# Five edits to the first part of a sparse graph-attention kernel: shared buffers, later degree counts, v beside A, a column-wise split, deeper loads

**Chip, cores, metric.** One core of a Trainium2 chip; the batches of runs used several chips, each with the kernel before beside it. The metric is the device time of one execution in microseconds (us). Lower is better.

## What the kernel computes

The reference is one graph-attention layer over 3327 nodes with 1024 features. It is cut here to what matters:

```python
h = jnp.maximum(_layernorm(x, axis=-1), 0.0)          # x: 3327 x 1024, float32
f = h @ Wf + bf
g = h @ Wg + bg
e = jax.nn.relu(f @ g.T)
scores = jnp.where(adj > 0, e, NEG)                    # adj: 3327 x 3327, int32, about 17 ones a row
attention = jax.nn.softmax(scores, axis=1)
x = x + attention @ (h @ W + bW)
```

Of the kernel before, what the change touches and what calls it, by code (L numbers as in the profile page):

```python
# [26 lines left out]
AHEAD = 3  # L27

# [260 lines left out]
def edge_path(ctx: ExitStack, tc: tile.TileContext, x, adj, Wf, bf, Wg, bg, W, bW, out, flag):  # L289
# [46 lines left out]
    sel3 = const.tile([3, 3], FP, name="sel3")  # L336
    make_identity(nc, sel3)
# [13 lines left out]
    def split3(pool, to, of):  # L351

        n = of.shape[1]
        rest = pool.tile([3, n], FP, name="rest")
        tc.keep_in_program_order(nc.vector.tensor_copy(rest, of))
        part = pool.tile([3, n], BF, name="part")
        acc = pool.tile([3, n], FP, name="part_acc")
        for i in range(3):
            nc.vector.tensor_copy(part, rest)
            if i == 0:  # L360
                nc.vector.tensor_scalar(acc, part, sel3[:, 0:1], None, op0=ALU.mult)
            else:
                nc.vector.scalar_tensor_tensor(acc, part, sel3[:, i : i + 1], acc, op0=ALU.mult, op1=ALU.add)
            if i < 2:
                nc.vector.tensor_sub(rest, rest, part)
        nc.vector.tensor_copy(to, acc)


    with ExitStack() as part1:
        pool1 = lambda name, bufs, **kw: part1.enter_context(tc.tile_pool(name=name, bufs=bufs, **kw))  # L370
        c1 = pool1("c1", 1)
        wrow = pool1("wrow", 2)
        wT = pool1("wT", 2)
        ln = pool1("ln", 3)
        lnj = pool1("lnj", 1)
        apool = pool1("adj", 2)
        kpool = pool1("key", 2)
# [4 lines left out]
        p_lst = pool1("p_lst", 1, space=PSUM)  # L382
        p_c = pool1("p_c", 1, space=PSUM)

# [5 lines left out]
        iotad = p_c.tile([P, NBIN], FP, name="iotad")  # L390
# [10 lines left out]
        deg = c1.tile([P, NT], FP, name="deg")  # L401
        cnt = c1.tile([P, NT], FP, name="cnt")
# [39 lines left out]
        def degrees(t):  # L442
            n = rows(t)
            a = apool.tile([P, N], I32, name="a")
            for b, m in pieces(t):
                nc.sync.dma_start(a[b : b + m], adj[t * P + b : t * P + b + m, :])
            r = kpool.tile([P, N], FP, name="r")
            nc.scalar.activation(r[:n], a[:n], AF.Relu, accum_out=deg[:n, t : t + 1])  # L448
            nc.gpsimd.tensor_mul(r[:n], r[:n], iotaj[:n])  # L449
            return r  # L450

        def edges(t, r):

# [9 lines left out]
            lst = p_lst.tile([P, KM], FP, name="lst")  # L463
# [9 lines left out]
            nc.vector.tensor_scalar(oh[:n, t, :], iotad[:n], dg[:n], None, op0=ALU.is_equal)  # L473

# [29 lines left out]
        bf3 = c1.tile([P, KD, 3], FP, name="bf3")  # L504
        bWf = c1.tile([3, O], FP, name="bWf")
        nc.gpsimd.dma_start(bfT, bf.rearrange("(k p) -> p k", p=P))
        nc.gpsimd.dma_start(bgT, bg.rearrange("(k p) -> p k", p=P))
        nc.gpsimd.dma_start(bWf, bass.AP(tensor=bW.tensor, offset=bW.offset, ap=[[0, 3], [1, O]]))
        nc.vector.tensor_copy(bf3, bfT[:, :, None].to_broadcast([P, KD, 3]))
# [6 lines left out]
        def make_A(c):  # L516
# [15 lines left out]
            nc.scalar.copy(A_sb[:, c, D : D + 1], ps[:, 0:1])  # L532

        def make_rows():

            ps = p_u.tile([P, P], FP, name="ps_u")
            for k in range(KD):
                nc.tensor.matmul(ps[:3, 0:1], bf3[:, k, :], bgT[:, k : k + 1], start=(k == 0), stop=(k == KD - 1))
            split3(c1, v3[:, D : D + 1], ps[:3, 0:1])
            for o in range(OH):  # L540
                ps = p_mm.tile([P, CB], FP, name="ps_A")
                for k in range(KD):
                    nc.tensor.matmul(  # L543
                        ps[:3], bf3[:, k, :], WgT[:, k, o * CB : (o + 1) * CB], start=(k == 0), stop=(k == KD - 1)
                    )
                split3(c1, v3[:, o * CB : (o + 1) * CB], ps[:3])
                split3(c1, bW3[:, o * CB : (o + 1) * CB], bWf[:, o * CB : (o + 1) * CB])

        for t in range(NT):
            r = degrees(t)  # L550
            normed(t)
            edges(t, r)
# [4 lines left out]
            elif t < 2 * KD:  # L557
                make_A(t - KD)
# [292 lines left out]
```

## The kernel before

The kernel does not compute 3327 x 3327 scores. Its first part goes once through the rows, in 26 tiles of 128. For each tile it normalises the rows of x and writes them to `hd` in DRAM. It also loads the rows of adj and turns them into "keys" (adj times column number). From these VectorE picks the neighbours' column numbers with Max8 instructions, eight largest values at a time, up to 40 a row. Beside that PE builds A = Wf Wg^T, so that a score becomes one dot product of (h A + v) with a neighbour's h. At the end of the first part the rows are sorted by degree; the sorted order is `perm`. The second part gathers each row's neighbours, computes the scores, the softmax and the output. The change leaves the second part alone.

The pieces of the first part that matter, with cuts marked by `# ...`:

```python
wrow = pool1("wrow", 2)
ln = pool1("ln", 3)          # row buffers: xt and its small companions
apool = pool1("adj", 2)
kpool = pool1("key", 2)
# ...
def normed(t):
    xt = ln.tile([P, D], FP, name="xt")
    # nc.sync.dma_start: load of x
    if t % 2:                                   # odd tiles: statistics on VectorE
        st = ln.tile([P, D // CB, 6], FP, name="st")
        for c in range(D // CB):
            nc.vector.bn_stats(st[:n, c, :], xt[:n, c * CB : (c + 1) * CB])
        mv = ln.tile([P, 2], FP, name="mv")
        nc.vector.bn_aggr(mv[:n], st[:n])
        nc.scalar.activation(nmr[:n], mv[:n, 0:1], AF.Copy, scale=-1.0)
        nc.scalar.activation(rstd[:n], mv[:n, 1:2], AF.Sqrt, bias=eps[:n])
    else:                                       # even tiles: two passes on ScalarE
        # ...
    nc.vector.reciprocal(rstd[:n], rstd[:n])
    nc.scalar.activation(nmr[:n], nmr[:n], AF.Copy, scale=rstd[:n])
    nc.scalar.activation(xt[:n], xt[:n], AF.Relu, bias=nmr[:n], scale=rstd[:n])
    # nc.scalar.dma_start: store to hd

def degrees(t):
    a = apool.tile([P, N], I32, name="a")
    # nc.sync.dma_start: load of adj
    r = kpool.tile([P, N], FP, name="r")
    nc.scalar.activation(r[:n], a[:n], AF.Relu, accum_out=deg[:n, t : t + 1])   # "the adj pass"
    nc.gpsimd.tensor_mul(r[:n], r[:n], iotaj[:n])                               # "the multiply"
    return r

def edges(t, r):
    for s in range(SEG):                                                        # "the scans"
        nc.vector.max(cand[:n, s * 8 : s * 8 + 8], r[:n, s * SW : min(N, (s + 1) * SW)])
    # ... list work on VectorE; then a product on PE and a masked sum on VectorE (rp)

for t in range(NT):
    r = degrees(t)
    normed(t)
    edges(t, r)
    # ... store_lists
    if t < KD:
        load_Wg(t)
    elif t < 2 * KD:
        make_A(t - KD)
# ... sort by degree, giving perm and final
make_rows()      # v on three partitions, and split3 of v and bW into three bf16 parts
```

Each engine gets its instructions in an order that is fixed when the kernel is built. "Emitted earlier" below means earlier in the program. The build interleaves neighbouring pieces. So where the order matters, it is read from a timeline.

## Time and profile before

| | before |
|---|---|
| median of 3 runs | 1437.71 us (1436.15 to 1441.19) |
| profiled run, span | 1436.2 us |
| first scan | 20.6 us |
| loop end (start of the prefix scan after the last tile) | 277.4 us |
| permutation known | 290.8 us |
| first gathered dot | 329.9 us |
| first dot to end | 1106.3 us |

These milestones are start times in the timeline of the profiled run and are used all through. The prediction below shows the stretches, the waits and the chain of the kernel before. Each line of a timeline is: start (us), duration (us), engine, line, operation, output<-inputs, shapes, and in brackets how long the engine idled before and who released it.

### The profile page before, as it was taken

Reading aid. Unit: us, or ns where it says so; the run is one execution under the profiler, and the core shown is the slowest. Engines: PE = TensorE matmul, PEld = TensorE weight load, DVE = VectorE, ACT = ScalarE, POOL = GpSimd, SP = SyncE. Lnnn points to the kernel's source line nnn. Section 1 sums busy time; section 2 is a strip of 40 time slices with the busy share of each in tenths; the row PEclk is TensorE's granted clock in tenths of the full one; section 3 lists DMA queues with packets and bytes.
Section 4 is the critical chain, followed back from the end, with each engine's and each line's share of the span. In section 5 each row is a group of like instructions: output and inputs, shape, how many; then the busy total and the mean of one; then the engine's idle time right before and its main releaser. Section 6 shows DMA issues by size and latency. Waiting matters only on the chain.

```text
span 1436.2 us, 13878 instructions
## 1 busy us (share of the span) xinstructions
PE 1160.7 (81%) x4242; PEld 657.3 (46%) x4242; DVE 1266.7 (88%) x2647; ACT 442.7 (31%) x673; POOL 873.6 (61%) x627
## 2 busy tenths in 40 slices
PE   1249899457087998999979888999999998999676
PEld 1225454034063665556455444555555554555332
DVE  3878888977979999998988889999999988999991
ACT  6666757301060444324122221222222111111100
POOL 8676776426756677665575556666676765666500
PEclk9999899769588999999989898999999998999788
DMA  8898887249768888896796668887787776787700
GB/s 340 292 348 294 325 302 260 86 140 402 236 224 310 310 315 276 302 314 206 279 324 210 230 261 281 292 286 271 266 287 258 257 254 228 252 275 256 263 30 32
DMA packets 97709, 372.51 MB, mean 259 GB/s; under 512 B 14265, under 2 KB 14681, under 8 KB 94297
## 3 DMA queue, kind: packets, MB, share of 16 engines
q0 software_dynamic: 79552, 286.86, 57.6%
q1 hardware_dynamic: 10860, 70.49, 13.4%
q10 hardware_dynamic: 7212, 14.18, 2.6%
q8 instruction: 35, 0.57, 0.2%
q14 instruction: 50, 0.41, 0.1%
HBM read 343.68 MB, written 27.80 MB: 259 GB/s over the span
## 4 chain that ended last, share of the span: by engine, by line
PE 35%; DVE 27%; issue 18%; POOL 10%; DMA 6%; ACT 3%; POOLq 0%; ACTq 0%; SPq 0%; DVEq 0%
PE ps_o L749 16%; DVE y L735 12%; PE ps_q L655 10%; POOL r L449 6%; DVE junk L672 5%; PE yT_ps L713 5%; DMA G<-hd,pi 4%; POOL G L627 4%; DVE cand L458 3%; PE ps_A L525 2%; ACT r L448 1%; PE ps_A L543 1%; DVE xp L757 1%; DVE sc L672 1%; DVE lst L465 1%
## 5 line engine op out<-in xcount | busy, mean ns | idle before, releaser
L627 POOL DMA_INDIRECT G<-hd,pi x468 | 560.8, 1198 | 316.6 <-ACT y L733 99.1
L672 DVE CUSTOM_DVE_ANT_0 junk<-G,q 128x1024 bf16<-128x1024 f32 x468 | 600.7, 1284 | 31.5 <-DMA G<-hd,pi 28.8
L655 PE MATMUL ps_q<-A_sb,hT 128*128 128x342 f32 x1248 | 394.5, 466 | 63.5 <-ACT q L657 53.5
L735 DVE SCALAR_TENSOR_TENSOR y<-G,sc,y 128x1024 f32<-128x1024 f32 x320 | 411.3, 1285 | 4.7 <-ACT y L733 2.9
L749 PE MATMUL ps_o<-W_sb,yT 128*128 128x512 f32 x832 | 387.1, 620 | 9.8 <-ACT yT L744 9.5
L655 PEld LDWEIGHTS ps_q<-A_sb,hT 128*128 128x128 f32 x1248 | 233.2, 194 | 183.4 <-ACT q L657 55.6
L749 PEld LDWEIGHTS ps_o<-W_sb,yT 128*128 128x128 f32 x832 | 161.0, 198 | 207.9 <-issue 189.1
L449 POOL TENSOR_TENSOR r<-r,iotaj 128x3327 f32<-128x3327 f32 (+1 forms) x26 | 187.8, 7232 | 73.1 <-ACT r L448 61.5
L458 DVE MAX8 cand<-r 128x8 f32<-128x208 f32 (+2 forms) x416 | 134.1, 361 | 39.8 <-POOL r L449 39.8
L657 ACT COPY q<-ps_q 128x342 f32<-128x342 f32 x78 | 32.8, 449 | 328.7 <-DVE sc L672 225.2
L729 ACT ACTIVATE G<-G,sc 128x1024 f32<-128x1024 f32 x122 | 129.0, 1136 | 0.0
L525 PE MATMUL ps_A<-WgT,WfT 128*128 128x512 f32 x256 | 120.3, 630 | 2.9 <-ACT WfT L499 2.9
L713 PE MATMUL yT_ps<-ident,G 128*128 128x128 f32 x976 | 116.4, 275 | 1.3 <-ACT G L729 1.3
L713 PEld LDWEIGHTS yT_ps<-ident,G 128*128 128x128 f32 x976 | 106.7, 141 | 13.2 <-ACT G L729 5.9
L639 ACT COPY hT<-ps_t 128x512 f32<-128x512 f32 x52 | 30.1, 593 | 192.1 <-PE ps_q L655 159.8
L744 ACT COPY yT<-yT_ps 128x512 f32<-128x512 f32 x52 | 27.8, 586 | 199.1 <-PE yT_ps L713 199.1
L525 PEld LDWEIGHTS ps_A<-WgT,WfT 128*128 128x128 f32 x256 | 50.8, 202 | 74.1 <-issue 64.7
L448 ACT ACTIVATE r<-a 128x3327 f32<-128x3327 int32 (+1 forms) x26 | 77.2, 2968 | 9.5 <-issue 5.4
L713 PE MATMUL yT_ps<-ident,y 128*128 128x128 f32 x208 | 33.8, 316 | 56.6 <-DVE y L735 35.7
L758 POOL DMA_INDIRECT out_dram<-xp,perm x25 | 31.7, 1268 | 56.9 <-DVE xp L757 50.9
L757 DVE TENSOR_TENSOR xp<-ps_o,xp 128x512 f32<-128x512 f32 x52 | 35.6, 685 | 34.2 <-PE ps_o L750 34.0
L713 PEld LDWEIGHTS yT_ps<-ident,y 128*128 128x128 f32 x208 | 28.0, 163 | 61.4 <-DVE y L735 38.5
(137 smaller groups left out, 748.7 us busy)
## 6 DMA issues: line engine op xcount, KB each, us to landing
a<-in_adj_dram SPq DMA_DIRECT2D x25, 1663.5 KB, 9.1
xt<-in_x_dram SPq DMA_DIRECT2D x25, 512.0 KB, 4.2
hd<-xt ACTq DMA_DIRECT2D x25, 512.0 KB, 5.6
G<-hd,pi POOLq DMA_INDIRECT x468, 6.1
wr<-in_L_gnn_Wg_dram SPq DMA_DIRECT2D x8, 512.0 KB, 6.0
wr<-in_L_gnn_Wf_dram SPq DMA_DIRECT2D x8, 512.0 KB, 5.0
W_sb<-in_L_gnn_W_dram SPq DMA_DIRECT2D x1, 4096.0 KB, 14.2
a<-in_adj_dram SPq DMA_DIRECT2D x1, 1455.6 KB, 9.6
```

Of the source, the lines that this page charges most:

```text
L448: nc.scalar.activation(r[:n], a[:n], AF.Relu, accum_out=deg[:n, t : t + 1])
L449: nc.gpsimd.tensor_mul(r[:n], r[:n], iotaj[:n])
L458: nc.vector.max(cand[:n, s * 8 : s * 8 + 8], r[:n, s * SW : min(N, (s + 1) * SW)])
L525: nc.tensor.matmul(ps, WfT[:, k, :], WgT[:, k, o * CB : (o + 1) * CB], start=(k == 0), stop=(k == KD - 1))
L627: nc.gpsimd.indirect_dma_start(out=to, out_offset=None, in_=table, in_offset=bass.IndirectOffsetOnAxis(ap=idx, axis=0),)
L655: nc.tensor.matmul(ps[:, :QB], hT[:, k, :], A_sb[:, k, o : o + QB], start=(k == 0), stop=False)
L672: nc.vector.tensor_tensor_reduce(junk, g, e["q"][:, :D], 1.0, e["q"][:, D : D + 1], op0=ALU.mult, op1=ALU.add, accum_out=e["sc"][:, k : k ...
L713: nc.tensor.matmul(e["yT"][:, c, :], g[:, c * P : (c + 1) * P], ident, is_transpose=True, start=(first and c % 4 == 0), stop=(last and c % ...
L729: nc.scalar.activation(g, g, AF.Copy, scale=p)
L735: nc.vector.scalar_tensor_tensor(y, g, p, y, op0=ALU.mult, op1=ALU.add)
L749: nc.tensor.matmul(ps, yT[:, k, :], W_sb[:, k, o * CB : (o + 1) * CB], start=(k == 0), stop=False)
L757: nc.vector.tensor_add(xo, e["o"][o], xo)
```

## The change

The intent is to let the loop run nearer to its engines' own limits, and to take a tail of small work off the path after the loop:

- adj and key share four buffers, so the adj pass works in place;
- the product and masked sum of a tile's degrees come four tiles after its list (`LAG = 4`);
- v is made along with A as columns, and the split into bf16 parts works on 17 columns of 128 partitions at tile 16, where it worked on rows of three partitions after the loop;
- the last two tiles run adj pass and multiply in halves;
- five row buffers in place of three, three weight-row buffers in place of two.

```diff
+LAG = 4
-        wrow = pool1("wrow", 2)
+        wrow = pool1("wrow", 3)
-        ln = pool1("ln", 3)
+        ln = pool1("ln", 5)
-        apool = pool1("adj", 2)
-        kpool = pool1("key", 2)
+        kpool = pool1("key", 4)
@@ degrees
-            a = apool.tile([P, N], I32, name="a")
+            r = kpool.tile([P, N], FP, name="r")
+            a = r.bitcast(I32)
-            nc.scalar.activation(r[:n], a[:n], AF.Relu, accum_out=deg[:n, t : t + 1])
-            nc.gpsimd.tensor_mul(r[:n], r[:n], iotaj[:n])
+            cuts = [0, SEG // 2 * SW, N] if t >= NT - 2 else [0, N]
+            for i, (b, e) in enumerate(zip(cuts, cuts[1:])):
+                to = deg[:n, t : t + 1] if not i else half[:n]
+                nc.scalar.activation(r[:n, b:e], a[:n, b:e], AF.Relu, accum_out=to)
+                nc.gpsimd.tensor_mul(r[:n, b:e], r[:n, b:e], iotaj[:n, b:e])
# ... (deg plus half)
@@ make_A
+            for k in range(KD):
+                nc.tensor.matmul(
+                    v_ps[:, c : c + 1], WgT[:, k, c * P : (c + 1) * P], bfT[:, k : k + 1],
+                    start=(k == 0), stop=(k == KD - 1),
+                )
@@ make_rows
# ... (split3 on 3 partitions removed)
+            for i in range(3):
+                nc.vector.tensor_copy(terms[:, i, :], cols)
+                if i < 2:
+                    nc.vector.tensor_sub(cols, cols, terms[:, i, :])
# ... (17 small products bring the parts back to three partitions)
@@ loop
             edges(t, r)
+            if t >= LAG:
+                counted(t - LAG)
# ...
+            if t == 2 * KD:
+                make_rows()
@@ after the sort
-        make_rows()
```

## The prediction, made before the changed kernel ran

> **What bounds the kernel now.** I read the page first, for the engines' shares over the 40 slices; then the table of busy time by stretches, to split the run; then the waits of the first 305 us, those of the DMA queues included; then the chain and the timeline around the end of the first part.
>
> The change touches only the first part (lists of neighbours, layer norm, A = Wf Wg^T, the permutation), which ends near 290 us; the first gathered dot of the second part starts at 329.88 us. The rest, 330 to 1436 us, runs the same code after the change. In the table of stretches the columns are PE, PEld, DVE, ACT, POOL (busy us and instructions), the granted clock, the share of the DMA engines and GB/s:
>
> ```profile
> 90.00:110.00 20.00, 13.34 (x28) 5.52 (x27) 14.32 (x73) 11.23 (x20) 14.45 (x2) 1.00 0.87 334
> 130.00:150.00 20.00, 18.84 (x69) 10.00 (x67) 16.45 (x83) 13.55 (x21) 14.45 (x2) 1.00 0.90 337
> 190.00:210.00 20.00, 19.79 (x65) 10.16 (x65) 14.03 (x67) 13.93 (x22) 12.24 (x2) 1.00 0.70 256
> 290.00:305.00 15.00, 0.92 (x25) 0.74 (x23) 13.27 (x35) 0.00 (x0) 4.08 (x4) 0.50 0.42 140
> ```
>
> No engine is full in the loop over the 26 row tiles. VectorE has 194.8 us of work in the 240 us from 30 to 270 us (sum over the stretches), 81%, at a period of 10 us per tile: 8.1 us of work a tile. GpSimd shows two multiplies of 7.23 us in most stretches of 20 us (14.45, x2). The DMA engines' share times 20 us, summed over 0 to 270 us, gives 217 us. So three resources could each go faster than 10 us a tile (8.1, 7.2, and 217/26 = 8.35 us), and something couples them. The waits say what (total us, times, longest; SPq is the queue that issues the loads of adj, x and the weights, in order):
>
> ```profile
> SPq L417 <- DMA hd<-xt: 147.3, 18, 15.9
> POOL r L449 <- ACT r L448: 61.5, 18, 8.1
> DVE cand L458 <- POOL r L449: 39.8, 17, 3.9
> ACT nmr L437 <- DVE rstd L436: 30.1, 11, 4.7
> ACT nmr L426 <- DVE mv L425: 16.4, 7, 4.2
> SPq L610 <- DVE bW L366: 24.7, 1, 24.7
> ```
>
> The load of x (L417) stands 147 of the loop's some 260 us until an old row buffer has been stored to hd: there are three such buffers. All later loads, adj included, stand behind it. A ring follows: store of hd, load of x, statistics on VectorE, ScalarE's nmr and its adj pass, GpSimd's multiply, the Max8 scans on VectorE, the next layer norm. The last row is a second matter, after the loop. VectorE then splits two rows of three partitions into bf16 parts; the memory of the first part is not free until that ends. The chain there (start, us, what):
>
> ```profile
> 287.77 0.78 DVE place L585
> 289.03 1.32 PE ps_u L591 x26
> 290.92 0.55 PE ps_u L538 x16
> 293.21 0.61 DVE rest L355
> ...
> 304.25 0.61 DVE rest L355
> 304.95 1.94 PE ps_t L638 x8
> 306.89 6.70 PE ps_q L655 x16
> ```
>
> The permutation is known at 290.8 us, yet the transposes of the first gathered rows start at 304.95[...]. The split as a whole runs until 315.3, and only then does the gather of the lists start:
>
> ```profile
> 315.58 0.95 POOL L627 DMA_INDIRECT pi<-pd,perm  x1 [7.13 <-DVE bW L366]
> ...
> 322.20 0.94 POOL L627 DMA_INDIRECT G<-hd,pi  x1 [3.17 <-issue]
> ```
>
> [...]the stretches here reach 374 GB/s at a share of 0.96, so the measurement puts the ceiling near 390 and I use the shares. [...]a subtraction on 3x512 takes 0.67 us[...], one on 3x1 0.14 us. So 17 columns on 128 partitions must be near the small end.
>
> **The change part by part.**
>
> *Five row buffers, three weight-row buffers.* The load of x waits for a store two tiles older than now, some 20 us earlier at the present period. The longest such wait is 15.9 us, so it should nearly vanish, and with it the queueing of adj loads.
>
> *Shared adj/key buffers.* Two adj plus two key buffers become four that serve both, the same memory. A buffer is held from the issue of its load to the last Max8: 9.1 us landing (12 when several loads are queued, my estimate), 3.2 ScalarE, 7.3 GpSimd with up to 4 of waiting, 5.5 for the scans mixed with list work: 25 to 32 us. Over four buffers that is 6.3 to 8 us a tile: just enough, without much to spare.
>
> *Degree counts four tiles behind.* The product of tile t with the triangle and its masked sum move behind the list of tile t+4. VectorE waits 7.8 us in all for that product and PE 43.8 us for its input, as PE works off A in blocks of 14 to 16.8 us. No instruction vanishes. I count 5 of VectorE's 45 us of loop idle here.
>
> *v along with A.* The row form took 32 products of 676 ns on PE (17.4 us). It becomes 64 fp32 products with one moving column, 128 records; the like-shaped group for u (128x1, x128) is busy 14.7 us with the records overlapping. PE in the loop is thus 3 us lighter or equal. PE is nearly full from 110 to 250 us (18.6 of 20), but starts A only near 98 us, when all of Wg has landed. With faster loads I put that at 70 to 75 us. Eight blocks of 18.5 us plus 1.8 each take 163 us: A ends near 235, before the loop does. So PE is not the bound, by 10 us or so.
>
> *Column-wise split at tile 16.* The split took 291.5 to 315.3 us, 23.8 us of VectorE. It becomes five operations on 17 columns, some 0.2 us each by the small ones above, plus six ScalarE copies (0.6 us at most each) and 17 small products, all inside the loop. VectorE gains 23 us; how much is on the path must be worked out (below).
>
> *Last two tiles in halves.* The scans of the last tile could start 3.6 us earlier (half of 7.21). But VectorE is busy with the tile before until 270.9 while the last multiply ends at 269.7. I count 1 us.
>
> **The sum.** Loop: from the first scan (20.6 us) to the last masked sum (277.0) it takes 256 us, 9.87 a tile. The floors are 8.35 (DMA) and 8.1 (VectorE); two bounds so near each other are not both met, and I choose 8.8: 229 us, ending at 249.5. Gain 27.5, plus 1 for the halves. From there to the permutation 13.8 us as now. From the permutation to the first dot it is 329.9 - 290.8 = 39.1 us now. After: gather of rows issued 0.3 us later and landed after 6.3 more, transposes and copies 1.8, the three products of q 17.2 (306.8 to 323.94), copy and start 0.9: 26.5 us. The lists (fifth or sixth on GpSimd at 1.25 us, 5.6 landing) and the first G (6.6 landing) come in about 21 us, so q is last. Gain 12.6. The sum is 41; of it I take off 2 for the new work in the loop and for reordering in the second part, whose 1106 us are bound by VectorE (949 of 1010 us busy from 400 to 1410 us) and should only shift. 1437.7 - 39 = 1399 us.
>
> **The rivals.**
> 1. *The loop is DMA-bound.* The share is already 0.96 in one stretch (374 GB/s), and the first 16 tiles carry weights (3.3 MB each, by the sizes in the page's DMA rows, against 2.75). Then loads run at full share but the loop gets only to 9.3 a tile; gain 15 + 12.6: 1410. For it: shares of 0.78 to 0.96. Against: the mean is 0.82, with gaps that follow the x wait.
> 2. *The ring through ScalarE stays.* ScalarE waits 46 us for VectorE's statistics and reciprocals, which queue behind scans in VectorE's order; deeper loads don't change that. Then the loop keeps 9.6 to 9.8 a tile and only the tail's 13 us remain: 1425, within 2%. Against: the waits for mv follow late x data (mv at 66.98 us comes right after an x load issued at 62.81).
> 3. *PE takes over.* If A starts no earlier than now, A with the v columns ends at 98 + 163 = 261 us, the split waits for it, and VectorE or ScalarE stand in order behind it: 1412.
> 4. *The floors are met* (8.4 a tile): 10 us more: 1388.
>
> **Range and chances.** The tail's gain of 12 us is nearly sure, as the instructions leave the path; the loop's lies between 5 and 38. That gives 1380 to 1421 for 8 in 10, middle 1399. Faster by over 2% means under 1409, a loop at 9.2 a tile or better: 0.78. Within 2%: 0.20. Slower: 0.02, only if the new order stalls the engines.
>
> **What would show it.** Right: the wait of x loads on hd under 40 us; Max8 scans under 9.1 us a tile; DMA share above 0.9 until 200 us; A starting before 80; first dot 26 to 28 us after the permutation, near 289 us in the run; from there to the end 1106 us within 8. Wrong: scans still waiting about 40 us for GpSimd and GpSimd 60 for ScalarE (rival 2); adj loads waiting for scans, or a full share at over 9.2 a tile (rival 1); the split's copies late behind A (rival 3); or a second part that has grown by more than 10 us and gives the gain back.

27.5 + 1 for the loop and 12.6 for the tail make 41, less 2 is 39, and 1437.7 - 39 = 1399 us. The step from the two floors to 8.8 a tile, and the worth of the buffers, are estimates. Three things that the trace of the kernel before does show: a subtraction takes 0.14 us on 3x1 and 0.67 on 3x512 (L365), an addition 0.69 on 128x512 (L757), so in these three the time goes with the columns and not with the partitions; PE's wait of 13.5 us before the transposes at 304.95 ends with VectorE's last copy out of `ps_A` (L355, from 304.18 to 304.85); and the loads of adj land after 6.7 to 16.0 us, 9.1 in the median.

## More of the kernel before

```profile
50.93 7.24 POOL L449 TENSOR_TENSOR r<-r,iotaj 128x3327 f32<-128x3327 f32 x1 [6.10 <-ACT r L448]
58.62 7.21 POOL L449 TENSOR_TENSOR r<-r,iotaj 128x3327 f32<-128x3327 f32 x1 [0.45 <-ACT r L448]
71.12 7.23 POOL L449 TENSOR_TENSOR r<-r,iotaj 128x3327 f32<-128x3327 f32 x1 [5.30 <-ACT r L448]
```

Look at the rhythm: one short gap, one long gap of 5 to 6 us, and 20.19 us (71.12 - 50.93) for two tiles. The long gap ends each time with ScalarE's adj pass. Something that spans two tiles sets the pace.

## The result and the profile after

The changed kernel took 1420.61 us (median of 4 runs, 1417.90 to 1422.87). The kernel before took 1438.85 us (median of 4, 1436.15 to 1441.19) on the same chip. The ratio is 0.9873, with a 95% interval of 0.9847 to 0.9899: a gain of 1.3%, within 2%. A ratio here is the mean time of one kernel's fast runs over that of the other's of the same rounds, so it is not quite the ratio of the medians. The output is correct.

| profiled runs, us | before | after | predicted for after |
|---|---|---|---|
| loop end | 277.4 | 272.8 | 249.5, less 1 for the halves |
| permutation | 290.8 | 285.1 | |
| permutation to first dot | 39.1 | 27.9 | 26.5 |
| first dot | 329.9 | 313.0 | near 289 |
| first dot to end | 1106.3 | 1105.9 | 1106 within 8 |

The part after the loop did what was predicted. The loop did not: it gave 4.6 us, where 28.5 were expected.

The same stretches as in the prediction, now of the kernel after (busy us and instructions of PE, PEld, DVE, ACT and POOL, then granted clock, DMA share, GB/s):

```profile
90.00:110.00 20.00, 17.08 (x47) 8.21 (x46) 17.01 (x85) 13.80 (x23) 15.18 (x3) 1.00 0.79 284
130.00:150.00 20.00, 18.59 (x49) 8.88 (x48) 17.10 (x85) 12.66 (x21) 14.02 (x3) 0.83 0.81 307
190.00:210.00 20.00, 18.74 (x66) 9.79 (x66) 16.82 (x87) 15.36 (x25) 14.91 (x3) 1.00 1.01 323
```

VectorE is a little fuller (14.32 to 17.01 in the first stretch), but no engine is full and the DMA share is not steadily high. The waits of the kernel after, over the first 305 us (total us, times, longest):

```profile
SPq L430 <- DVE cand L446: 72.4, 10, 9.7
...
SPq L400 <- DMA hd<-xt: 13.7, 6, 5.6
...
POOL r L436 <- ACT r L435: 53.1, 18, 6.0
...
DVE cand L446 <- POOL r L436: 35.6, 15, 3.7
...
ACT nmr L420 <- DVE rstd L419: 22.7, 9, 5.9
...
ACT nmr L409 <- DVE mv L408: 15.2, 6, 4.0
```

The load of x (L400) waits 13.7 us for stored rows, where it waited 147.3. That edit worked as a mechanism. But the queue now stands elsewhere: the load of adj (L430) waits 72.4 us for the scans to release a shared buffer. And the waits between the engines have hardly moved: GpSimd for ScalarE 53.1 (61.5 before), VectorE for GpSimd 35.6 (39.8 before).

The tail, from the chain that ended last (start, us, what):

```profile
283.30 1.32 PE ps_u L603 x26
284.62 10.04 issue
294.66 1.94 PE ps_t L649 x8
```

The split is gone from here. Between the sort's product and the first transposes lies the gather of the rows (10.04 us, listed as issue), then the transposes and the three products of q, the last of which ScalarE copies at 312.53.

### The profile page after: what moved, and what is told of

The parts are those of the page before. It is cut to its first block, busy times and chain, and to the rows that moved or that the text cites. A ratio compares the mean times of both kernels' runs of the same rounds, so it can differ in the third digit from the quotient of the medians.

```text
span 1418.9 us, 14086 instructions
## 1 busy us (share of the span) xinstructions
PE 1176.7 (83%) x4355; PEld 686.1 (48%) x4355; DVE 1252.2 (88%) x2602; ACT 444.5 (31%) x686; POOL 872.4 (61%) x628
## 4 chain that ended last, share of the span: by engine, by line
PE 28%; DVE 25%; issue 22%; POOL 15%; DMA 6%; ACT 2%; POOLq 0%; ACTq 0%; SPq 0%; DVEq 0%
PE ps_o L760 14%; DVE y L746 13%; POOL r L436 10%; PE ps_q L666 8%; DVE junk L683 6%; PE yT_ps L724 4%; POOL G L638 4%; DMA G<-hd,pi 4%; DVE cand L446 2%; PE ps_A L519 1%; DVE xp L768 1%; DVE sc L683 1%; DMA pi<-pd,perm 1%; ACT r L435 1%; PE ps_o L761 1%
## 5 line engine op out<-in xcount | busy, mean ns | idle before, releaser
L666 PE MATMUL ps_q<-A_sb,hT 128*128 128x342 f32 x1248 | 395.9, 467 | 58.1 <-ACT q L668 44.5
L760 PE MATMUL ps_o<-W_sb,yT 128*128 128x512 f32 x832 | 388.2, 621 | 10.2 <-ACT yT L755 9.9
L436 POOL TENSOR_TENSOR r<-r,iotaj 128x3327 f32<-128x3327 f32 (+4 forms) x28 | 188.6, 6742 | 67.1 <-ACT r L435 53.1
L446 DVE MAX8 cand<-r 128x8 f32<-128x208 f32 (+2 forms) x416 | 134.2, 359 | 35.6 <-POOL r L436 35.6
L435 ACT ACTIVATE r<-r 128x3327 f32<-128x3327 int32 (+4 forms) x28 | 77.5, 2766 | 0.1
L768 DVE TENSOR_TENSOR xp<-ps_o,xp 128x512 f32<-128x512 f32 x52 | 35.6, 685 | 36.0 <-PE ps_o L761 35.7
```

What stands on the lines that cost most here:

```text
L435: nc.scalar.activation(r[:n, b:e], a[:n, b:e], AF.Relu, accum_out=to)
L436: nc.gpsimd.tensor_mul(r[:n, b:e], r[:n, b:e], iotaj[:n, b:e])
L666: nc.tensor.matmul(ps[:, :QB], hT[:, k, :], A_sb[:, k, o : o + QB], start=(k == 0), stop=False)
L760: nc.tensor.matmul(ps, yT[:, k, :], W_sb[:, k, o * CB : (o + 1) * CB], start=(k == 0), stop=False)
L768: nc.vector.tensor_add(xo, e["o"][o], xo)
```

## The ring, read from the timeline after

The timeline of the kernel after from 49 to 71 us shows what sets the pace. I put the lines that follow one another by cause in one fence; the lines between them are left out.

```profile
49.92 7.26 POOL L436 TENSOR_TENSOR r<-r,iotaj 128x3327 f32<-128x3327 f32 x1 [5.19 <-ACT r L435]
...
57.22 0.38 DVE L446 MAX8 cand<-r 128x8 f32<-128x208 f32 x1 [3.74 <-POOL r L436]
...
64.56 0.67 DVE L406 BATCH_NORM_STATS2 st<-xt 128x6 f32<-128x512 f32 x1
...
66.20 0.18 DVE L408 BATCH_NORM_AGGREGATE mv<-st 128x2 f32<-128x12 f32 x1
...
66.42 0.20 ACT L409 ACTIVATE nmr<-mv 128x1 f32<-128x1 f32 x1 [3.05 <-DVE mv L408]
...
66.91 2.98 ACT L435 ACTIVATE r<-r 128x3327 f32<-128x3327 int32 x1
...
70.05 7.25 POOL L436 TENSOR_TENSOR r<-r,iotaj 128x3327 f32<-128x3327 f32 x1 [5.23 <-ACT r L435]
```

Follow it step by step. GpSimd's multiply ends at 57.18 and releases VectorE's scans at 57.22. VectorE works through scans and list work; the statistics of the next odd tile stand behind them in its order and come out as mv at 66.38. ScalarE has waited 3.05 us for mv. Only then can it go on to the next adj pass, which stands behind `nmr<-mv` in its order although it needs nothing of it. The adj pass releases GpSimd at 70.05, after 5.23 us of idling. From multiply to multiply that is 7.26 + 9.2 (scans to mv) + 3.67 (mv to multiply): 20.13 us for two tiles. In the kernel before the same two multiplies lay 20.19 us apart. This stretch shows the rhythm most clearly. From 149 to 242 us the gaps of the kernel after are shorter and less regular, and two tiles take 18 to 20 us; that part was not followed step by step.

So my theory became this. **The ring** GpSimd, VectorE, ScalarE, GpSimd is closed by the in-order queues and was there before; load buffers do not touch it. That is rival 2 of the prediction. The experiments test it against three others: that the shared buffers cost what the load buffers gave; that PE with A is the bound; and that the DMA engines or VectorE have simply no more to give.

## The experiments

18 runs were made. The milestones come from one profiled run each. The changed kernel, run again unchanged as a control (`e18`), ended its loop at 269.0 us against 272.8, so 4 us of loop end is the spread of one and the same kernel, and smaller differences of single profiles prove nothing. The two timelines show where these 4 us come from: they agree within 0.4 us until 247 us, then one small cast of the split takes 3.53 us in one run and 0.17 us in the other, and all that follows is shifted (see e7). The kernel before, run beside them on the same chip, has medians of 1437.6 to 1439.9 us in all batches but one. The batch of e13 to e16 ran on a slower chip (before: 1507.22 us), where the second part is longer; of those runs I use ratios and the times of the loop, whose start (first scan near 20 us, A from 87 to 95 us) is as elsewhere.

| run | loop end | permutation to first dot | first dot to end | median | ratio to before [95%] |
|---|---|---|---|---|---|
| before | 277.4 | 39.1 | 1106.3 | 1438.85 | 1 |
| after | 272.8 | 27.9 | 1105.9 | 1420.61 | 0.9873 [0.9847, 0.9899] |
| e18 after again | 269.0 | 28.4 | 1108.7 | 1420.98 | 0.9877 [0.9845, 0.9909] |
| e1 few load buffers | 276.7 | 27.1 | 1111.4 | 1430.17 | 0.9932 [0.9903, 0.9962] |
| e2 v and split alone | 282.3 | 27.0 | 1109.4 | 1434.46 | 0.9972 [0.9953, 0.9991] |
| e3 adj pass ahead | 251.9 | 28.6 | 1105.4 | 1401.65 | 0.9748 [0.9720, 0.9775] |
| e4 adj pass and norm ahead | 269.9 | 28.3 | 1106.9 | 1420.25 | 0.9889 [0.9849, 0.9929] |
| e5 before, adj pass ahead | 267.2 | 40.2 | 1106.6 | 1425.72 | 0.9902 [0.9873, 0.9930] |
| e6 no lag | 271.3 | 27.0 | 1108.9 | 1423.23 | 0.9895 [0.9863, 0.9928] |
| e7 split after the loop | 268.6 | 28.4 | 1108.8 | 1419.30 | 0.9864 [0.9840, 0.9888] |
| e8 e3 and e7 together | 247.7 | 28.0 | 1107.9 | 1398.42 | 0.9722 [0.9684, 0.9760] |
| e9 all norm sums on ScalarE | 295.5 | 27.2 | 1108.9 | 1445.15 | 1.0051 [1.0015, 1.0087] |
| e10 adj and key apart | 271.0 | 28.1 | 1114.3 | 1427.16 | 0.9915 [0.9895, 0.9935] |
| e11 no halves | 275.6 | 28.2 | 1108.0 | 1427.34 | 0.9916 [0.9896, 0.9936] |
| e12 e8, A early | 268.0 | 28.2 | 1112.1 | 1423.55 | 0.9891 [0.9855, 0.9928] |
| e17 complete cut | 245.4 | 28.4 | 1107.6 | 1400.05 | 0.9748 [0.9708, 0.9788] |
| e13 incomplete cut (slow chip) | 272.0 | 49.0 | 1154.0 | 1484.76 | 0.9847 [0.9787, 0.9907] |
| e14 statistics cut (slow chip) | 266.4 | 34.4 | 1151.7 | 1474.33 | 0.9788 [0.9704, 0.9872] |
| e15 reciprocals cut (slow chip) | 269.9 | 48.8 | 1152.9 | 1479.85 | 0.9825 [0.9750, 0.9900] |
| e16 e8 without the lag (slow chip) | 256.7 | 48.6 | 1162.3 | 1481.15 | 0.9828 [0.9779, 0.9877] |

### The parts of the change, one by one

**e1: the changed kernel with the old load buffers.**

```diff
-        wrow = pool1("wrow", 3)
+        wrow = pool1("wrow", 2)
-        ln = pool1("ln", 5)
+        ln = pool1("ln", 3)
```

> The changed kernel with three row buffers and two weight-row buffers again, all else kept. My theory: the 147 us wait of the x loads was off the path (VectorE waited 1.9 us for x data before the change), so the time stays within 4 us of the changed kernel: 1417 to 1425 us, though the wait of x loads on stores comes back to over 60 us. Rival, my prediction's step: the row buffers carry what the loop gained; then it is 5 us or more slower than the changed kernel, 1425 to 1430 us.

Measured: loop end 276.7, median 1430.17. My expectation (1417 to 1425 us) missed, and the rival written beside it, the prediction's own step, came true in its number: without the load buffers the loop ends within 1 us of the kernel before (277.4). They are worth 4 to 8 us of loop (against the two runs of the kernel after), far from the prediction's 27.5 but not nothing; the intervals of the two ratios don't overlap. The profiled run's second part is 5.5 us longer than after's with the same order of instructions, so part of the 9.6 us between the medians may be spread. In the waits of e1 the wait of the x load is back, but this time the consumer waits too:

```profile
SPq L400 <- DMA hd<-xt: 167.7, 21, 17.4
...
DVE st L406 <- DMA xt<-in_x_dram: 11.7, 6, 5.0
```

In the kernel before, the same pair was 147.3 us and this, which the prediction did not look at:

```profile
DVE st L423 <- DMA xt<-in_x_dram: 1.9, 2, 1.5
```

This is the lesson in one line. The load of x waited 147.3 us for a free buffer, and nobody waited for the x that came of it: VectorE only 1.9 us in two instances, beside one first wait of 7.1 us on ScalarE at the start. (PE did wait for the rows of Wg, whose loads stand behind x in the same queue: 32.0 us before, 12.3 after. Yet A began at 94.0 and 93.2 us.) So beside a queue that stands, look up whether its consumer stands.

**e2: the kernel before with v along A and the column split alone** (the change with `LAG = 0`, without halves, and with the old buffers). The edit against the kernel after:

```diff
-LAG = 4
+LAG = 0
-        wrow = pool1("wrow", 3)
+        wrow = pool1("wrow", 2)
-        ln = pool1("ln", 5)
+        ln = pool1("ln", 3)
-        kpool = pool1("key", 4)
+        apool = pool1("adj", 2)
+        kpool = pool1("key", 2)
-            a = r.bitcast(I32)
+            a = apool.tile([P, N], I32, name="a")
-            cuts = [0, SEG // 2 * SW, N] if t >= NT - 2 else [0, N]
+            cuts = [0, N]
```

> Only the part about the rows of v and bW: v along with A, the column-wise split at tile 16, the merged PSUM tile[...]; counts, buffers and whole multiplies as before the change. Theory: the tail's 11 us (permutation to first dot 28 us in place of 39) are nearly the whole gain, so 1424 to 1429 us, with the last masked sum within 4 us of the kernel before (277 us). Rival: the loop's parts carry more; then 1430 us or above.

Measured: from the permutation to the first dot 27.0 us, so this part alone makes the whole tail gain of 12 us. But the loop ends at 282.3, 4.9 us later than before. The work moved into the loop was not free there: in e2's own trace a cast of the split stands 4.02 us on VectorE from 250.93 us, until GpSimd's multiply ends (see e7). And e2 as a whole gained 4 us by the medians.

**e6: the changed kernel without the lag.**

```diff
-LAG = 4
+LAG = 0
```

> The changed kernel with the degree counts straight behind each list again. The lag removed VectorE's waits for the product (7.8 us before, 1.4 after), but PE now waits 36.9 us for the masked sums in place of 15.4. Theory: the ring hides both, so the end of the loop stays within 4 us of 272.8 us and the time within 5 of 1420.6. Rival, my prediction's 5 us for this part: 277 us or later, 1425 or more.

Measured: loop end 271.3, between the two runs of the kernel after. The waits of PE for the masked sum fell (8.5 us against 36.9 with the lag), but those for `oh`, the other input of the product, rose (50.0 against 8.0), so PE waited more in all and the end of the loop did not follow. In this kernel the lag is worth nothing that can be measured.

**e10: adj and key buffers apart again**, two and two.

```diff
-        kpool = pool1("key", 4)
+        apool = pool1("adj", 2)
+        kpool = pool1("key", 2)
-            a = r.bitcast(I32)
+            a = apool.tile([P, N], I32, name="a")
```

> The changed kernel with two adj and two key buffers again in place of four shared. In the changed kernel the adj loads wait 72 us for scans on the shared buffers, and no engine waits for adj data, so sharing is off the path in either direction: loop end within 4 us of 272.8 us. Rival (sharing carried the loop's gain): 277 us or later. Rival (sharing holds the loop back): 268 us or earlier.

Measured: loop end 271.0, again between the two runs of after, though the adj load no longer waits for the scans (it waits 81.0 us for ScalarE in their place, 39.0 + 27.9 + 14.1). So the sharing neither helps nor harms the loop. That the standing queue itself costs nothing is seen on the other side: the waits of the kernel after have no instance of ScalarE waiting for adj data. The median (two runs) is 6.5 us higher; the profiled run has it in the second part (1114.3 us), which this edit does not touch by itself. Why it is longer there I did not find out.

**e11: no halves.**

```diff
-            cuts = [0, SEG // 2 * SW, N] if t >= NT - 2 else [0, N]
+            cuts = [0, N]
```

> The changed kernel with whole multiplies in the last two tiles. My estimate was 1 us. In the changed kernel the scans of the last tile do wait for its first half and the split stands between; so 2 to 5 us later, 275 to 278 us. If the halves cost as much as they give: within 2 us of 272.8.

Measured: loop end 275.6, 2.8 us after that of the kernel after, with the size that was expected, though within the spread of single profiles. It may not be the halves as such: one cast of the split stood 5.79 us behind a whole multiply here (3.53 us behind a half in the kernel after).

**e7: make_rows (with the split) after the loop.**

```diff
-            if t == 2 * KD:
-                make_rows()
# ...
         store_lists(20, NT)
+        make_rows()
```

> The changed kernel with the split into bf16 rows after the loop in place of tile 16. In the changed kernel one of its casts stands 3.5 us on VectorE at 247.9 us, and its copies stand on ScalarE in front of the last tile's adj pass. Theory: the loop's end comes 3 to 6 us earlier than 272.8, and the split hides beside the ranking, so the first dot comes 28 us or less after the permutation: 1413 to 1418 us. Rival: the split lies on the path again and the first dot comes later than 30 us after the permutation; then 1420 us or more.

Measured: loop end 268.6, median 1419.30, a difference from after of 1 us, in the noise. What the placement at tile 16 can cost is seen in the timeline of e3, which has the same placement:

```profile
230.56 0.16 DVE L543 TENSOR_TENSOR cols<-cols,terms 128x17 f32<-128x17 f32 x1
...
231.08 3.68 POOL L436 TENSOR_TENSOR r<-r,iotaj 127x1664 f32<-127x1664 f32 x1 [5.83 <-ACT r L435]
231.13 3.67 DVE L543 TENSOR_TENSOR cols<-cols,terms 128x17 f32<-128x17 f32 x1
```

The same subtraction of 17 columns takes 0.16 us alone and 3.67 us when it starts 0.05 us after GpSimd's multiply (half a tile, hence 3.68 us), and both end together (234.76 and 234.80). The trace shows the times and no cause. In the kernel after it was the cast of the same 17 columns, beside a multiply that runs from 247.68 to 251.36 us:

```profile
247.86 3.53 DVE L541 CAST terms<-cols 128x17 bf16<-128x17 f32 x1
```

The prediction had 0.2 us for each of these. Such a stall is also in e2 (4.02 us), e10 (3.68) and e11 (5.79); in e6, e17 and the second run of the kernel after, each VectorE instruction of the split took under 0.2 us; a cast of e6 that starts at 249.73, 0.01 us before a multiply, took 0.16. Nor does every VectorE instruction stand beside a multiply: in the kernel after, the nine Max8 scans that start from 57.77 to 61.71 us, beside the multiply of 57.60 to 64.82, take 0.35 to 0.37 us each, and the one just before it (57.22) 0.38. Behind the cast stand PE's small products and ScalarE's copies of v, and behind these in ScalarE's order the last adj passes. ScalarE waited 4.48 us for those products in the kernel after and 0.85 us in its second run: these are the 3.8 us between their loop ends.

### Opening the ring

**e3: the adj pass of tile t+1 is emitted before the layer norm of tile t.** Nothing else: the same instructions, buffers and loads.

```diff
+        r = {0: degrees(0)}
         for t in range(NT):
-            r = degrees(t)
+            if t + 1 < NT:
+                r[t + 1] = degrees(t + 1)
             normed(t)
-            edges(t, r)
+            edges(t, r.pop(t))
```

> The changed kernel with the adj pass of tile t+1 (load, ScalarE pass, GpSimd multiply) put ahead of the layer norm of tile t in the program. Theory: the loop is a ring of in-order queues: GpSimd's multiply of tile t (7.2 us), VectorE's scans and list work and then the statistics of tile t+1 (9.2), ScalarE's nmr and adj pass of t+2 (3.6), 20 us for two tiles. With the adj pass no longer behind the statistics, GpSimd's waits for ScalarE fall from 53 to under 25 us, the scans end 15 to 30 us earlier, and the time is 1392 to 1407 us. Rival A (DMA-bound or buffer-bound): the waits of the adj loads for scans grow instead, and the time stays within 5 us of 1420. Rival B (PE and A bound it): the split's copies wait for A, 1412 or more.

Measured: loop end 251.9, median 1401.65, ratio 0.9748. Moving one call gave 17 to 21 us of loop (against the two runs of the kernel after), where the five edits together gave 4.6 to 8.4. GpSimd's timeline in e3:

```profile
34.32 14.46 POOL L436 TENSOR_TENSOR r<-r,iotaj 128x3327 f32<-128x3327 f32 x2 [0.27 <-ACT r L435]
51.10 14.44 POOL L436 TENSOR_TENSOR r<-r,iotaj 128x3327 f32<-128x3327 f32 x2 [2.32 <-ACT r L435]
```

The multiplies run in pairs ("x2") and the pairs start 16.78 us apart, where the kernels before and after needed 20.19 and 20.13. The gap of 5 us is down to 2.3. This is 8.4 us a tile: it is the DMA floor of the prediction (8.35), and indeed in this stretch the DMA engines are at a share of 1.00 to 1.02, with 410 to 416 GB/s. Over the whole loop it is 8.93 us a tile. The waits of e3 that answer to those above:

```profile
POOL r L436 <- ACT r L435: 39.6, 13, 5.8
...
DVE cand L446 <- POOL r L436: 20.2, 13, 7.0
```

ScalarE's two waits for VectorE are 12.7 us (mv) and 10.2 us (reciprocals) here, against 15.2 and 22.7 in the kernel after.

**e5: the same one move in the kernel before.**

```diff
+        r = {0: degrees(0)}
         for t in range(NT):
-            r = degrees(t)
+            if t + 1 < NT:
+                r[t + 1] = degrees(t + 1)
             normed(t)
-            edges(t, r)
+            edges(t, r.pop(t))
```

> The kernel before, with nothing of the change but the adj pass of tile t+1 ahead of the layer norm of tile t. If the ring of queues bound the loop already before the change, its scans end earlier here too: last masked sum at 255 to 268 us in place of 277, time 1415 to 1430 us. Rival: this order needs the change's buffers (four shared adj/key, five rows); then the scans end within 5 us of 277 and the time stays at 1433 us or more.

Measured: loop end 267.2, 10.2 us earlier than before, with the wait of the x load on hd still at 129.2 us. So the ring bound the loop of the kernel before as well, and 129 us of standing queue did not prevent this gain. ScalarE's two waits for VectorE fell from 46.5 to 21.0 us and VectorE's for GpSimd from 39.8 to 24.4; GpSimd's for ScalarE did not fall (64.3 us, 61.5 before), so here the ring is opened only in part. With the ring open the five edits are worth more: e3, which has them, ends its loop 15 us before e5. Which of the five does that was not taken apart.

**e8: e3 and e7 together**, and the best version found.

```diff
+        r = {0: degrees(0)}
         for t in range(NT):
-            r = degrees(t)
+            if t + 1 < NT:
+                r[t + 1] = degrees(t + 1)
             normed(t)
-            edges(t, r)
+            edges(t, r.pop(t))
# ...
-            if t == 2 * KD:
-                make_rows()
# ...
         store_lists(20, NT)
+        make_rows()
```

> Adj pass one tile ahead, and the split after the loop. With the adj pass ahead the loop ended at 251.9 us, but from 226 us on it waited for the end of A, the split and the last half passes behind it. Theory: another 4 to 8 us: loop end 244 to 248, 1392 to 1398 us. Rival: A on PE (end at 226 us) plus the list work left holds the end, so within 2 us of the run with the adj pass ahead alone.

Measured: loop end 247.7, median 1398.42 us (1393.03 to 1403.02), ratio 0.9722 [0.9684, 0.9760], correct. It beats both kernels. It lies 3 us under e3 by the medians of different batches; the intervals overlap, so this last step is not shown.

**e4: adj pass and layer norm of t+1 both ahead of the scans of t.**

```diff
+        r = {0: degrees(0)}
+        normed(0)
         for t in range(NT):
-            r = degrees(t)
-            normed(t)
-            edges(t, r)
+            if t + 1 < NT:
+                r[t + 1] = degrees(t + 1)
+                normed(t + 1)
+            edges(t, r.pop(t))
```

> As the run before, and the layer norm of t+1 too ahead of the scans of t. Theory: VectorE's statistics then come before the scans that wait for GpSimd, so ScalarE doesn't wait for them either: as good as or better than the run before, 1388 to 1407 us. Rivals as before: within 5 us of 1420.

A miss: loop end 269.9, median 1420.25. The statistics are emitted ahead of the scans, but every queue moved together. ScalarE waited 24.0 us for mv (15.2 after) and 25.5 for PE's blocks of A (16.4 after): A started later, at 97.8, and ended at 252.8. The work emitted earlier came in front of other work in the queues that it touches.

### Can the ring be opened at ScalarE or PE instead?

**e9: all sums of the layer norm on ScalarE**, so that VectorE has no statistics.

```diff
-            if t % 2:
+            if False:
```

> The changed kernel with the layer norm's sums of the odd tiles on ScalarE too, as the even tiles have them; VectorE keeps the reciprocals only. A second way to open the ring: ScalarE no longer waits for mv (15 us) in front of an adj pass. It adds some 2.3 us to ScalarE in each of 13 tiles and takes 1.4 from VectorE. Theory: the loop ends at 255 to 268 us in place of 272.8, the time is 1404 to 1416 us. Rival A: buffers or DMA bound the loop, and it ends within 4 us of 272.8. Rival B: the reciprocals behind the scans (22.7 us of ScalarE waits) hold the ring alone: also within 4 us.

A miss in the other direction: loop end 295.5, ratio 1.0051. ScalarE still waits for VectorE's reciprocal on every tile, now 56.3 us (22.7 after), and has two more passes of 1.0 and 1.15 us in every odd tile ahead of its adj pass. Taking work off VectorE lengthened the ring.

**e12: e8 with Wg loaded two blocks a tile in the first four tiles**, so that A starts early.

```diff
-            if t < KD:
-                load_Wg(t)
-            elif t < 2 * KD:
-                make_A(t - KD)
+            if t < KD // 2:
+                load_Wg(2 * t)
+                load_Wg(2 * t + 1)
+            elif t < KD // 2 + KD:
+                make_A(t - KD // 2)
```

> Adj pass one tile ahead, split after the loop, and Wg loaded two rows of blocks a tile in the first four tiles, so that A starts earlier. In the run without this PE worked off A without a gap from 160 to 228 us and the chain lay on it; A started at 87 us. Theory: A starts at 60 to 70 us and ends near 205, VectorE is the bound, and the loop ends 3 to 8 us before 247.7: 1389 to 1396 us. Rival: the DMA engines are full until 110 us, so the first tiles' adj comes later by what Wg takes, and the loop ends within 2 us of 247.7 or later.

A miss, and a useful one: A ran from 68.6 to 211.5 us, in e8 from 87.2 to 226.1, and yet the loop ended 20 us later than in e8. The loss is made early: the seventh multiply starts at 76.4 us here and near 58.1 in e8, and from there to the end of the loop the two take 192 and 190 us. So 15 us of earlier A bought nothing, which speaks against rival 3. Why the first tiles are late is not shown; ScalarE's wait for reciprocals was 29.5 us against 10.5 in e8, and the granted clock was lower, too (0.82 against 0.91 over 30 to 270 us). The DMA shares that the rival's "full until 110 us" speaks of are 0.96 to 1.02 from 30 to 110 us in e8.

### Cutting the ring

**e13: ScalarE takes its shift and scale from constants.** VectorE still computes the statistics and reciprocals, but nobody waits for their values. The result is wrong (relative error 0.082).

```diff
-                nc.scalar.activation(nmr[:n], mv[:n, 0:1], AF.Copy, scale=-1.0)
-                nc.scalar.activation(rstd[:n], mv[:n, 1:2], AF.Sqrt, bias=eps[:n])
+                nc.scalar.activation(nmr[:n], zo[:n, 0:1], AF.Copy, scale=-1.0)
+                nc.scalar.activation(rstd[:n], zo[:n, 1:2], AF.Sqrt, bias=eps[:n])
# ...
-            nc.vector.reciprocal(rstd[:n], rstd[:n])
+            inv = ln.tile([P, 1], FP, name="inv")
+            nc.vector.reciprocal(inv[:n], rstd[:n])
```

> The changed kernel with ScalarE freed of VectorE's layer-norm results, all instructions kept: nmr and rstd of the odd tiles are taken from constants, and the reciprocals go to a tile that nobody reads. The result is wrong on purpose (the rows are scaled by the deviation in place of its inverse). Theory: with those waits gone (54 us in the changed kernel: 22.7 reciprocals, 15.2 and 10.9 statistics) ScalarE runs ahead, GpSimd's waits for it fall under 30 us and the loop ends at 245 to 258 us in place of 272.8; time 1393 to 1406 us. If the loop still ends within 5 us of 272.8, the ring through VectorE's small results is not the cause.

A miss: loop end 272.0, no gain at all. (The 54 us of the expectation are 48.8 by its own parts.) Taken at face value this refutes the ring. The timeline says why it does not (ScalarE's and VectorE's lines in order of time):

```profile
64.03 0.67 DVE L409 BATCH_NORM_STATS2 st<-xt 128x6 f32<-128x512 f32 x1
...
64.74 1.24 ACT L425 ACTIVATE xt<-xt,nmr,rstd 128x1024 f32<-128x1024 f32 x1 [2.01 <-DVE st L409]
...
65.89 2.96 ACT L439 ACTIVATE r<-r 128x3327 f32<-128x3327 int32 x1
```

ScalarE normalises in place. It does not write xt before VectorE has read it for the statistics (it waits 2.01 us for that here), and VectorE reads it behind its scans. The value was cut, but the order was not: the wait for data had become a wait for the right to overwrite, 18.2 us in all, with the adj pass standing behind it as before. The eleventh multiply starts at 108.1 us, as in the kernel after (108.4).

That is not the whole reason. Later e13 did gain: its 24th multiply starts at 224.5 us, 8.4 us ahead of the kernel after. It lost this at the end, where ScalarE waited 7.6 and 3.3 us for the last blocks of A (which ended at 242.7) and 6.2 us for the products of the split, with the last adj passes behind these in its order. That is rival 3's mechanism, at work in the last tiles.

**e14 and e15: the two halves of this cut alone** (statistics; reciprocals), also wrong, with relative errors of 0.052 and 0.091. e14:

```diff
-                nc.scalar.activation(nmr[:n], mv[:n, 0:1], AF.Copy, scale=-1.0)
-                nc.scalar.activation(rstd[:n], mv[:n, 1:2], AF.Sqrt, bias=eps[:n])
+                nc.scalar.activation(nmr[:n], zo[:n, 0:1], AF.Copy, scale=-1.0)
+                nc.scalar.activation(rstd[:n], zo[:n, 1:2], AF.Sqrt, bias=eps[:n])
```

e15:

```diff
-            nc.vector.reciprocal(rstd[:n], rstd[:n])
+            inv = ln.tile([P, 1], FP, name="inv")
+            nc.vector.reciprocal(inv[:n], rstd[:n])
```

> Only the statistics' dependence cut (odd tiles take constants), the reciprocals kept; wrong on purpose. If the statistics in front of the adj pass alone close the ring, as I read the changed kernel's trace: loop end 255 to 265 us. If the reciprocals alone do: within 4 us of 272.8.

> Only the reciprocals' dependence cut, statistics kept; wrong on purpose. By the theory the statistics still stand in front of every second adj pass: loop end 262 to 272 us, less gained than by cutting the statistics. Rival: the reciprocals are the ring, 258 us or earlier.

Loop ends of 266.4 and 269.9. With the statistics cut, the wait for reciprocals rose from 22.7 to 48.2 us; with the reciprocals cut, that for mv rose from 15.2 to 20.7 us (the part of it that is put down to another releaser went from 10.9 to 9.1). The eleventh multiply starts at 109.6 and 109.2 us, no earlier than after. So up to there neither half alone opens the ring; that the in-place write takes part here is argued, not shown.

**e17: the complete cut.** e13, and ScalarE writes the normalised rows to tiles of their own (two of them, one row buffer fewer). Wrong (0.082).

```diff
+        lno = pool1("lno", 2)
# ...
-            nc.scalar.activation(xt[:n], xt[:n], AF.Relu, bias=nmr[:n], scale=rstd[:n])
+            xo = lno.tile([P, D], FP, name="xo")
+            nc.scalar.activation(xo[:n], xt[:n], AF.Relu, bias=nmr[:n], scale=rstd[:n])
```

> Wrong on purpose, as e13_cut_both is: ScalarE takes its shift and scale from constants and not from VectorE's statistics and reciprocals, which are still computed. New against e13: ScalarE writes the normalised rows into tiles of their own (two of them, with four row buffers in place of five), so that this write no longer waits for VectorE to have read the rows. ScalarE then waits for VectorE nowhere in the layer norm. If the ring VectorE, ScalarE, GpSimd sets the loop, the loop ends at 235 to 258 us (after: 272.8), GpSimd waits for ScalarE's adj pass under 35 us (after: 53) and VectorE for GpSimd's product under 25 us (after: 36). Rival: the ring closes through PE, by ScalarE's copies of A in order with the adj passes (24 us of waits in e13): then the loop ends at 262 to 275 us and ScalarE's waits for A stay at 20 us or more. Second rival, the engines themselves (VectorE's 8.1 us a tile, or GpSimd's 7.2[...]): the loop ends at 262 or later with VectorE busy over 95% of it.

Measured: loop end 245.4, median 1400.05, ratio 0.9748. The loop is 24 to 27 us shorter than in the two runs of after, one of which ran on the same chip. Waits, and one stretch, of e17:

```profile
POOL r L442 <- ACT r L441: 35.6, 12, 5.7
...
ACT A_sb L528 <- PE ps_A L525: 18.1, 11, 4.0
...
DVE cand L452 <- POOL r L442: 10.4, 9, 2.9
```

```profile
90.00:110.00 20.00, 19.79 (x66) 10.15 (x65) 19.93 (x96) 16.04 (x24) 15.39 (x4) 1.00 1.01 413
```

VectorE's wait for GpSimd is down from 35.6 to 10.4 us, GpSimd's for ScalarE to 35.6 (0.6 over what I had written). ScalarE's waits for A stayed, at 18.1 us, so they were not what held the loop. And in this stretch, with the ring cut, VectorE is busy 19.93 of 20 us and the DMA share is 1.01: the floors of the prediction are reached. On one chip, the kernel after (e18) and the same kernel with ScalarE's layer norm freed of VectorE (e17) end their loops at 269.0 and 245.4 us: that shows what held the loop. The eleventh multiply starts at 92.3 us, 16 us earlier than in e13 and after; in e3 near 92.9. That both halves of the cut are needed, the value and the right to write, rests on e13, which ran on another chip and whose last tiles were held by A, so it is shown for these first ten tiles only. Separate tiles with the values kept were not run; there the write still waits for VectorE's reciprocal, so I would expect nothing of them.

**e18: the control on the chip of e17.** The kernel after, unchanged.

> The changed kernel once more, unchanged, as the control for the chip that e17_cut_complete runs on. Every theory expects the loop to end at 268 to 277 us, the first gathered dot 27 to 28.5 us after the permutation, and a ratio to the kernel before of 0.983 to 0.992.

Loop end 269.0, ratio 0.9877, as expected.

**e16: e8 without the lag.** The edit against e8:

```diff
-LAG = 4
+LAG = 0
```

> Adj pass one tile ahead, split after the loop, counts without the lag. In the changed kernel the lag was worth nothing (loop end 271.3 without it, 272.8 with it). With the loop at 247.7 us, PE waits 20.5 us for masked sums; so within 4 us of it either way: loop end 244 to 252, 1394 to 1403 us. If the lag is needed once the ring is open: 256 or later.

Loop end 256.7, 9 us later than e8's, on another chip. The lag, worth nothing in e6, seems to be worth something once the ring is open; since the pair did not run on one chip, I call this likely, not shown.

## Why the prediction was right and where it failed

1. *The tail: right.* It put the first dot 26.5 us after the permutation and the gain at 12.6. Measured: 27.9 and 11.2 us (the gather of the rows took 3 us longer than counted, the three products of q 1.3 us less), and 27.0 to 28.6 in each variant with the new split on a chip of the usual speed. e2 shows that the new v and split alone do it.
2. *The second part: right.* 1105.9 us, 0.4 from the kernel before.
3. *The loop: the failed step.* The prediction wrote "I choose 8.8: 229 us, ending at 249.5". The two floors were sound: e17, with the ring cut, ran 8.65 us a tile ((245.4 - 20.5) / 26), and e8 8.78 from its own first scan. The ceiling near 390 GB/s, which its sum does not use, was too low: e17 reached 413 in the stretch shown above, at a share of 1.01. What failed was the step from a standing queue to its worth. It read "The load of x (L417) stands 147 of the loop's some 260 us" as the link that couples the engines, without asking who waits for x. The answer was 1.9 us on VectorE. The changed loop ran at 9.70 us a tile ((272.8 - 20.7) / 26), against 9.88 before ((277.4 - 20.6) / 26).
4. *The ring was named wrongly.* The prediction's ring ran through the store of hd and the load of x. The real one has no transfer in it: multiply, scans, statistics, adj pass, 20.1 us for two tiles before and after. Rival 2 had it ("ScalarE waits 46 us for VectorE's statistics and reciprocals, which queue behind scans in VectorE's order; deeper loads don't change that") with a loop of 9.6 to 9.8 a tile and a time of 1425. It was set aside by a wrong reading: "mv at 66.98 us comes right after an x load issued at 62.81". Counted in order, the load issued at 62.81 is the seventh tile's. The mv at 66.98 is the sixth tile's, whose x load was issued at 51.38, 14 us before the statistics read it (65.34). The timeline of GpSimd over two periods would have told, too. The 1420.6 us measured sit at the upper edge of the range.
5. *The signs that it named.* The wait of x loads on hd fell under 40 us: yes (13.7), and this sign meant little for the time (4 to 8 us, e1). A before 80: no (93.2). DMA share over 0.9 until 200 us: no. Scans waiting about 40 us for GpSimd and GpSimd 60 for ScalarE: 35.6 and 53.1, rival 2's sign. Adj loads waiting for scans, the sign given to rival 1, came too (72.4 us), but e10 removed that wait and gained nothing. Rival 3's sign came in part: the split's copies stood late behind a stalled cast, which cost up to 4 us (e7, e18). A itself took 148.7 us in place of the 163 counted.
6. *Small terms.* The work in the loop was taken as 2 us together with reordering; in e2 it is 4.9, with a stall of 4.0 us between VectorE and GpSimd as one visible piece. The halves (1 us expected, 2.8 measured in one pair of profiles) and the lag are too small to separate. The load buffers gave 4 to 8 us.

What adds up: loop end 277.4 before, 282.3 with the new v and split alone (e2), 276.7 with lag, sharing and halves added (e1), 272.8 or 269.0 with the load buffers (after, and again). Each step is known to some 4 us only.

Left open: what sets the pace from 149 us on, where the ring was not followed; why an instruction of the split can stand on VectorE until GpSimd's multiply ends (3.67 us in e3); why e4, e9 and e12 close the ring just where they do (only their waits were read, no step of theirs was cut by itself); why the second part is 5 to 8 us longer in the profiled runs of e1 and e10; and how much of the remaining waits in e8 (GpSimd 33.4 us for ScalarE) is DMA-bound and how much is still ring.

## What to carry to other kernels

A queue that stood before its buffers cost little here, as the consumer of its data did not stand (147.3 us against 1.9): look up both waits before you size a gain from more buffers. When no engine is full and the gaps repeat, take the timeline of one engine over two or three periods, follow the ring of "released by" until it comes back, and see whether an instruction in it only stands behind another without needing it; moving that one call was worth 17 to 21 us of loop here (e3), the load buffers 4 to 8 (e1). When you cut a dependence to prove it, cut the write-after-read as well as the value, or the cut may show nothing (the eleventh multiply at 108.1 us in e13, with the write in place, and at 92.3 in e17); and look where a cut run loses what it gained.
